# Two transforms moved inside the rounds of a spectral stage

## The chip, the cores and the metric

The kernel runs on one core of one Trainium2 chip. The metric is the device time in microseconds of one execution. Before the change three timed runs gave 10308.48, 10305.58 and 10307.53 us, a median of 10307.53.

## The reference, cut to what matters

The reference is a two-layer model on 4 images of 64 x 64 positions with 128 channels, in float32. Layer 0 is a selective scan in four directions and a mixture of experts; layer 1 is a mixing of sums and a spectral layer. Only the last one is touched:

```
def _stu_conv(phi, u, n):                        # n = 8192
    Vf = rfft(phi, n=n, axis=0)                  # 16 filters of 4096 taps
    Uf_p, Uf_m = rfft(u, n=n, axis=1), rfft(u * sgn3, n=n, axis=1)
    U_plus  = irfft(Vf[None, :, :, None] * Uf_p[:, :, None, :], n=n, axis=1)[:, :sl]
    ...
out = einsum('btkd,k,kde->bte', U_plus, s, Mpp) + einsum('btkd,k,kde->bte', U_minus, s, Mpm)
```

So a sequence of 4096 tokens is convolved with 16 filters, the results (once plain, once with alternating signs) go through one 128 x 128 matrix for each filter, and all are summed.

## The kernel before

The kernel turns the order round. For each frequency the 32 filter values and the 32 matrices are first combined into one 128 x 128 matrix, and the transformed tokens are multiplied by that. `spectrum()` does this for all frequencies, as the last stage but one. The stages before it (scans with pieces of other work dealt between them, the experts, the first part of the transform in `to_slots`) end at about 8736 us; `endings()` follows and does the last part of the inverse transform.

`spectrum()` is a loop of 32 rounds, `i = 0 ... 31`; each handles two slots (`FB = 2`) of 64 frequencies. A round issues these parts:

- `load(i + 2)` and `load_back(i - 1)`: loads, all from SyncE's queue (L1461, L1464, L1466, L1546, L1551).
- `taps_of(i)` makes the matrices, in 16 steps (`C // 8`). A step is eight matmuls with 32 rows (L1495) into a pair of PSUM buffers, and two copies of 128 x 1024 elements from these into `wt`, one with the elements woven (L1506), one plain (L1509).
- `forward(i + 1)`: the second part of the forward transform of the next round's tokens. For each slot there are four matmuls (L1474) and a copy into `ut` through the helper at L1456. Both slots share one PSUM buffer.
- `backward(i - 1)`: the first part of the inverse transform of the previous round's product. It is four matmuls of 512 columns (L1559) into one PSUM buffer, one copy into `zo`, and two stores to `zd` (L1564).
- `product(i)`: eight groups of 16 matmuls (L1524), tokens times matrices, each group followed by a copy into `zs`; every second copy is followed by four stores to `zf` (L1538).

`forward` and `backward` do not stand before or after `taps_of` but inside it. A dictionary `between` holds, for a step's number, a function that `taps_of` calls behind that step's copies (L1510).

Three things set the order and the waits around this.

First, buffers. All matmuls of the stage write to one pool of four PSUM buffers, `sp_ps` (L1436), each of two banks. `taps_of` takes two for a step, `forward` and `backward` one each, `product` one for each group. `wt` has one buffer (L1444): the first copies of a round wait until `product` of the round before has read it, and `product` reads all of it. `ut`, `vt`, `u1`, `fq`, `zq` and `gq` have two buffers, `zo` one and `zs` three.

Second, the copies. `copy()` (L1451) hands them out in turn to ScalarE and VectorE. A round has 32 + 2 + 1 + 8 = 43, an odd number; so in one round VectorE takes the first copy of each step and in the next ScalarE does. In what follows these are V rounds and S rounds.

Third, the framework orders each engine's instructions by a plan of its own, close to the program's order but not the same. VectorE and ScalarE work off their copies in that order, and SyncE its loads and stores.

Of the kernel before, what the change touches and what calls it, by code (L numbers as in the profile page):

```python
# [18 lines left out]
B, H, W, C = 4, 64, 64, 128  # L19
# [82 lines left out]
def kernel(  # L102
# [1330 lines left out]
    def spectrum():  # L1433

        with tc.tile_pool(name="sp", bufs=2) as sp, tc.tile_pool(
# [12 lines left out]
            def banks():  # L1448
                return sps.tile([P, 2, 512], F32, name="sp_ps", tag="ps")
# [5 lines left out]
            def out(dst, src):  # L1455
                copy()(dst, src)  # L1456

            def load(i):
                vt[i] = sp.tile([P, FB, 2 * BP], F32, name="vt")
                for g in range(4):  # L1460
                    nc.sync.dma_start(vt[i][g * KK : (g + 1) * KK], vd[:, FB * i : FB * (i + 1)])  # L1461
                for q in range(FB * i, FB * (i + 1)):
                    u1[q] = sp.tile([P, B, C], F32, name="u1")
                    nc.sync.dma_start(u1[q], ud[q])  # L1464
                    fq[q] = sp.tile([P, 2 * BP], F32, name="fq")
                    nc.sync.dma_start(fq[q], fq_d[q])  # L1466

            def forward(i):
                ps = banks()
                ut[i] = sp.tile([P, FB, BP, 2, B], F32, name="ut")  # L1470
                for s in range(FB):
                    q = FB * i + s
                    for b in range(B):
                        nc.tensor.matmul(  # L1474
                            ps[:, s, b * 2 * BP : (b + 1) * 2 * BP],
                            u1[q][:, b, :],
                            fq[q],
                            start=True,
                            stop=True,
                        )  # L1480
                    out(
                        ut[i][:, s].rearrange("d m u b -> d b (m u)"),
                        ps[:, s].rearrange("d (b n) -> d b n", b=B),
                    )

            def taps_of(i, between):
                for j in range(C // 8):
                    pair = [banks(), banks()]
                    for t in range(2):
                        for g in range(4):  # L1490
                            rows = slice(g * KK, (g + 1) * KK)
                            bank = pair[g // 2][:, g % 2]
                            woven = bank.rearrange("d (n t) -> d t n", t=2)[:, t]
                            plain = bank[:, t * 256 : (t + 1) * 256]
                            nc.tensor.matmul(  # L1495
                                woven if (g // 2 + j) % 2 else plain,
                                taps[rows, j, t, :],
                                vt[i][rows].rearrange("k s n -> k (s n)"),
                                start=True,
                                stop=True,  # L1500
                            )
                    for h in range(2):
                        dst = wt[:, 2 * j + h]
                        if (h + j) % 2:
                            src = pair[h].rearrange("d g (n t) -> d n g t", t=2)
                            copy()(dst.rearrange("d n (g t) -> d n g t", g=2), src)  # L1506
                        else:
                            src = pair[h].rearrange("d g (t n) -> d n (g t)", t=2)
                            copy()(dst, src)  # L1509
                    if j in between:  # L1510
                        between[j]()

            def product(i):
                for s in range(FB):
                    q = FB * i + s
                    for m in range(0, BP // 4, 4):
                        if m % 8 == 0:
                            zs = sp.tile([P, BP // 8, 2, C], F32, name="zs", bufs=3)
                        ps = banks()
                        for k in range(4):  # L1520
                            w0 = ut[i][:, s, 4 * (m + k) : 4 * (m + k) + 4]
                            for g in range(4):
                                n = 2 * (s * BP + 4 * (m + k) + g)
                                nc.tensor.matmul(  # L1524
                                    ps[32 * g : 32 * g + 32, k // 2, (k % 2) * 256 :][:, 0:256],
                                    w0.rearrange("d m u b -> d (m u b)"),
                                    wt[:, :, n : n + 2, :].rearrange("d a w e -> d w a e"),
                                    start=True,
                                    stop=True,
                                )  # L1530
                        out(
                            zs[:, m % 8 : m % 8 + 4].rearrange("z m w e -> z (m w e)"),
                            ps.rearrange("z k n -> z (k n)"),
                        )
                        if m % 8 == 0:
                            continue
                        for g in range(4):
                            nc.sync.dma_start(  # L1538
                                zf[q].rearrange("(m g) z n -> z g m n", g=4)[:, g, m - 4 : m + 4],
                                zs[40 * g : 40 * g + 8].rearrange("z m w e -> z m (w e)"),  # L1540
                            )

            def load_back(i):
                for q in range(FB * i, FB * (i + 1)):
                    zq[q] = sp.tile([P, B, 2, C], F32, name="zq")
                    nc.sync.dma_start(  # L1546
                        zq[q].rearrange("k b w e -> k (b w e)"),
                        zf[q].rearrange("m (u b) n -> (m u) (b n)", u=2),
                    )
                    gq[q] = sp.tile([P, 2, 2 * BP], F32, name="gq")  # L1550
                    nc.sync.dma_start(gq[q], gq_d[q])  # L1551

            def backward(i):
                ps = banks()
                zo = sp.tile([P, FB, B * C], F32, name="zo", bufs=1)
                for s in range(FB):
                    q = FB * i + s
                    for w in range(2):
                        nc.tensor.matmul(  # L1559
                            ps[:, s, :], gq[q][:, w, :], zq[q][:, :, w, :], start=(w == 0), stop=(w == 1)  # L1560
                        )
                out(zo, ps)
                for s in range(FB):
                    nc.sync.dma_start(  # L1564
                        zd[FB * i + s].rearrange("r p b e -> (r p) (b e)"), zo[:, s, :]
                    )
# [5 lines left out]
            for i in range(n):  # L1572
                between = {}
                if i + 2 < n:
                    load(i + 2)
                if i + 1 < n:
                    between[5] = lambda: forward(i + 1)
                if i >= 1:
                    load_back(i - 1)
                    between[10] = lambda: backward(i - 1)  # L1580
                taps_of(i, between)
                product(i)
            load_back(n - 1)
# [71 lines left out]
    with ExitStack() as c0:  # L1655
# [113 lines left out]
        for s in range(-5, total + 2):  # L1769
            i = max(s, 0) // N  # L1770
# [138 lines left out]
    side.pop("pool").close()  # L1909
    weights.close()  # L1910
    spectrum()
    endings()

# [73 lines left out]
```

## Time and profile before

| | us |
|---|---|
| median of three runs | 10307.53 |
| the profiled execution's own time | 10298.26 |
| its span in the trace | 10296.2 |
| up to 8736 (all before the spectral stage) | 8736.0, TensorE's granted clock 0.79 |
| 8736 to 10139 (the spectral stage) | 1403.0, clock 0.99; TensorE busy 1272.8, VectorE 816.5, ScalarE 694.4, GpSimd 0 |
| 10139 to the end (`endings`) | 157.2, clock 0.76, DMA engines busy 91% |
| one L1495 / L1524 / L1474 / L1559 matmul instruction in the trace | 0.374 / 0.379 / 0.275 / 0.592 |
| a `wt`, `zs` or `zo` copy on VectorE / on ScalarE | 1.22 / 1.01 |
| a `ut` copy on either | 1.06 |

The profile is one execution taken by the hardware profiler. Time in it is counted from the start of its span. A line of its views names the start, the length, the engine, the source line, the operation, what is written and read, how many instructions were merged, and, in brackets, how long the engine had been idle and what ended that. TensorE appears as PE, VectorE as DVE, ScalarE as ACT, GpSimd as POOL, SyncE's queue as SPq. Each float32 matmul shows as two records, so eight matmuls appear as x16. Matmuls overlap, so the time of a group is less than the sum of its records.

### The profile page before, as it was taken

The page shows a single profiled execution, that of the slowest core. Times are in us where ns is not written, and L with a number is a line of the kernel's source. Part 1 is how long each engine was busy: PE and PEld are TensorE (multiplying, and loading weights), DVE is VectorE, ACT ScalarE, POOL GpSimd, SP SyncE. Part 2 cuts the span into 40 slices and gives each one's busy share as a digit, 9 for nine tenths or more (in the row PEclk, how much of TensorE's full clock was granted, in tenths as well). Part 3 has the DMA queues.
Part 4 walks back from the last instruction along what each step waited for, and adds up shares of the span by engine and source line. Part 5 has one row for each costly group of instructions (what it writes and reads, how often), then busy time and mean ns, then how long its engine had stood idle before and what let it go on. Part 6 is the DMA issues. An engine that isn't in the chain of part 4 may idle for free. (4 is left out here: it accounts for less than half of the span.)

```text
span 10296.2 us, 137906 instructions
## 1 busy us (share of the span) xinstructions
PE 7631.4 (74%) x45570; PEld 4960.9 (48%) x45570; DVE 8537.4 (83%) x7103; ACT 6159.3 (60%) x11847; POOL 6493.4 (63%) x5948
## 2 busy tenths in 40 slices
PE   7676777667767767787767776767777767999996
PEld 3444444445543545444544554543555445666662
DVE  0899999989999999998999999999999951555553
ACT  4665766656755566675765666765576644554551
POOL 1677777878877778877877788877788741000000
PEclk9787787768777878788878887868877776999998
DMA  2556556657656645656756656756646663233336
GB/s 90 169 170 207 178 187 212 191 180 225 196 172 202 214 155 174 200 180 207 250 173 225 202 162 218 232 167 219 213 155 199 193 215 95 80 87 86 87 87 161
DMA packets 941918, 1806.03 MB, mean 175 GB/s; under 512 B 88184, under 2 KB 506648, under 8 KB 937624
## 3 DMA queue, kind: packets, MB, share of 16 engines
q1 hardware_dynamic: 941208, 1797.22, 54.7%
q8 instruction: 366, 6.00, 0.2%
q14 instruction: 344, 2.82, 0.1%
HBM read 1554.66 MB, written 242.22 MB: 175 GB/s over the span
## 5 line engine op out<-in xcount | busy, mean ns | idle before, releaser
L1846 POOL TENSOR_TENSOR hh<-hh,bc 128x1024 f32<-128x1024 f32 x2048 | 4886.8, 2386 | 384.9 <-DVE hh L1836 151.0
L1836 DVE TENSOR_TENSOR_SCAN hh<-da,hst,db 128x512 f32<-128x512 f32 x3584 | 4393.1, 1267 | 281.5 <-PE y L1872 30.1
L1872 PE MATMUL y<-ident,hh 128*128 128x128 f32 x16384 | 2723.2, 321 | 1524.8 <-POOL hh L1846 1429.0
L1786 ACT ACTIVATE da<-dl,aneg 128x512 f32<-128x512 f32 x4096 | 2781.8, 717 | 1543.7 <-DVE hh L1836 1531.2
L1872 PEld LDWEIGHTS y<-ident,hh 128*128 128x128 f32 x16384 | 2259.0, 166 | 2486.4 <-POOL hh L1846 1868.7
L1830 DVE TENSOR_TENSOR db<-du,bc 128x1024 f32<-128x1024 f32 x1920 | 2365.2, 1232 | 97.7 <-ACT du L1767 19.2
L1845 POOL COPY hst<-hh 128x2 f32<-128x2 f32 x1792 | 365.9, 204 | 1037.9 <-DVE hh L1836 937.0
L1495 PE MATMUL sp_ps<-vt,taps 32*128 32x256 f32 x8192 | 638.1, 405 | 52.3 <-DVE wt L1509 19.7
L1836 DVE TENSOR_TENSOR_SCAN hh<-da,db 128x512 f32<-128x512 f32 x512 | 597.0, 1208 | 38.4 <-PE y L1872 5.8
L1495 PEld LDWEIGHTS sp_ps<-vt,taps 32*128 32x128 f32 x8192 | 438.1, 185 | 245.6 <-DVE wt L1506 63.0
L440 PE MATMUL cv_ps<-xh,diag 128*128 128x512 f32 x1152 | 525.8, 599 | 1.8 <-ACT sg_v L382 0.9
L1524 PE MATMUL sp_ps<-wt,ut 128*32 128x256 f32 x8192 | 448.7, 379 | 45.2 <-DVE wt L1509 22.7
L1830 DVE TENSOR_TENSOR db<-dx,bc 128x1024 f32<-128x1024 f32 x128 | 179.3, 1401 | 297.9 <-POOL dx L1714 285.8
L1686 PE MATMUL dt_ps<-dts,dtw 8*128 8x512 f32 x512 | 378.9, 844 | 52.8 <-ACT sg_v L382 35.5
L1506 DVE COPY wt<-sp_ps 128x1024 f32<-128x1024 f32 x257 | 314.4, 1223 | 123.6 <-PE sp_ps L1495 112.2
L1509 DVE COPY wt<-sp_ps 128x1024 f32<-128x1024 f32 x255 | 311.3, 1221 | 121.9 <-PE sp_ps L1495 115.4
L1711 PE MATMUL dl_ps<-ex,ident 128*128 128x512 f32 x512 | 315.3, 704 | 121.9 <-POOL ex L1705 121.8
L1524 PEld LDWEIGHTS sp_ps<-wt,ut 128*32 128x32 f32 x8192 | 318.7, 110 | 172.6 <-ACT wt L1506 28.7
L1705 POOL TENSOR_TENSOR ex<-ex,dx 128x1024 f32<-128x1024 f32 x128 | 302.0, 2360 | 107.6 <-DMA bc<-bc_d 72.5
L1509 ACT COPY wt<-sp_ps 128x1024 f32<-128x1024 f32 x257 | 260.2, 1012 | 178.4 <-PE sp_ps L1495 169.4
L1456 DVE COPY zs<-sp_ps 128x1024 f32<-128x1024 f32 x128 | 156.5, 1222 | 241.8 <-PE sp_ps L1524 235.6
L1714 POOL TENSOR_TENSOR dx<-dl,xc 128x1024 f32<-128x1024 f32 x128 | 302.5, 2363 | 69.3 <-ACT dl L1712 62.8
(289 smaller groups left out, 9915.6 us busy)
## 6 DMA issues: line engine op xcount, KB each, us to landing
bc<-bc_d SPq DMA_DIRECT2D x2048, 512.0 KB
xc<-xc_d SPq DMA_DIRECT2D x128, 512.0 KB
y_d<-ys SPq DMA_DIRECT2D x128, 512.0 KB
w1t<-in_w_dram SPq DMA_DIRECT2D x96, 512.0 KB
w2t<-in_w_dram SPq DMA_DIRECT2D x192, 256.0 KB
xc_x<-xc_d SPq DMA_DIRECT2D x64, 512.0 KB
yk<-y_d SPq DMA_DIRECT2D x128, 256.0 KB
yk<-y_d SPq DMA_DIRECT2D x256, 128.0 KB
```

The lines of the kernel that those rows point to most:

```text
L440: nc.tensor.matmul(ps, diag[:, h, t, :], xh[:, 8 * g + dy : 8 * g + dy + 8, dx : dx + W], start=(t == 0), stop=(t == 8),)
L1495: nc.tensor.matmul(woven if (g // 2 + j) % 2 else plain, taps[rows, j, t, :], vt[i][rows].rearrange("k s n -> k (s n)"), start=True, stop= ...
L1509: copy()(dst, src)
L1524: nc.tensor.matmul(ps[32 * g : 32 * g + 32, k // 2, (k % 2) * 256 :][:, 0:256], w0.rearrange("d m u b -> d (m u b)"), wt[:, :, n : n + 2, ...
L1686: nc.tensor.matmul(ps, dtw[:, k, h * P : (h + 1) * P], dts, start=True, stop=True)
L1711: nc.tensor.matmul(ps, ident, t[:, h], start=t is dl, stop=t is w)
L1786: i_act = nc.scalar.activation(das[t][:, h, :], sizes[t // N][0][:, h, :], AF.Exp, scale=aneg[:, tk, h, t % N : t % N + 1],)
L1830: nc.vector.tensor_mul(db, src, bcs[s][:, 0:1, :].to_broadcast([P, 2, SC]))
L1836: i_dve = nc.vector.tensor_tensor_scan(o, d0, d1, init, ALU.mult, ALU.add)
L1845: nc.gpsimd.tensor_copy(hsts[t // N][:, :, t % N], hhs[t][:, :, last])
L1846: i_pool = nc.gpsimd.tensor_mul(hhs[t], hhs[t], bcs.pop(t)[:, 1:2, :].to_broadcast([P, 2, SC]))
L1872: i_pe = nc.tensor.matmul(ys[c][:, q, h, :], hhs[t][:, h, q * P : (q + 1) * P], ident, is_transpose=True, start=(n == 0 and k > 0 and q % ...
```

## The change

In the loop of `spectrum()` two keys of `between` change. `forward(i + 1)` is called behind step 0 of `taps_of(i)` in place of step 5, and `backward(i - 1)` behind step 15, the last, in place of step 10. What the two functions do is as it was.

```diff
@@ -1574,10 +1574,10 @@
                 if i + 2 < n:
                     load(i + 2)
                 if i + 1 < n:
-                    between[5] = lambda: forward(i + 1)
+                    between[0] = lambda: forward(i + 1)
                 if i >= 1:
                     load_back(i - 1)
-                    between[10] = lambda: backward(i - 1)
+                    between[C // 8 - 1] = lambda: backward(i - 1)
                 taps_of(i, between)
                 product(i)
             load_back(n - 1)
```

In the order in which the changed program issues TensorE's instructions, the second half of the forward stands among the matmuls of step 1. On SyncE's queue the `vt` loads now stand ahead of the `gq` loads and the `zd` stores; before, they stood behind them.

## The prediction

> **What bounds the kernel now.** I read the whole page first, then busy time by stretch, then three views of one pair of rounds: TensorE in order of time, the chain that ended last, VectorE in order of time. The change sits in the spectral stage, which is 32 rounds. Cutting at the starts of `product` gives the stage its clock and load:
>
> ```profile
> 8767.36:9071.22 303.86, 277.14 (x3753) 188.66 (x3753) 177.96 (x150) 152.31 (x151) 0.00 (x0) 1.00 0.31 86
> 9374.05:9677.80 303.75, 278.10 (x3753) 189.81 (x3754) 178.06 (x150) 152.42 (x151) 0.00 (x0) 0.99 0.32 86
> ```
>
> Columns: the stretch, its length, then busy time of TensorE matmuls, weight loads, VectorE, ScalarE, GpSimd, then granted clock, DMA share, GB/s. In seven rounds (303.86 us) TensorE is busy 277.14 us; about 9% of the stage is TensorE waiting, and that is all that reordering can win. Clock and DMA leave room.
>
> TensorE in order of time, one round (start, duration, line, tiles, count, idle before it):
>
> ```profile
> 9027.65 14.02 PE L1524 MATMUL sp_ps<-wt,ut 128*32 128x256 f32 x256 [1.42 <-DVE wt L1509]
> 9041.60 1.15 PE L1495 MATMUL sp_ps<-vt,taps 32*128 32x256 f32 x16
> 9043.85 6.97 PE L1495 MATMUL sp_ps<-vt,taps 32*128 32x256 f32 x80 [1.10 <-ACT wt L1509]
> 9050.75 1.16 PE L1474 MATMUL sp_ps<-fq,u 128*128 128x128 f32 x8
> 9051.83 0.70 PE L1495 MATMUL sp_ps<-vt,taps 32*128 32x256 f32 x4
> 9053.05 1.16 PE L1474 MATMUL sp_ps<-fq,u 128*128 128x128 f32 x8 [0.51 <-ACT ut L1456]
> ...
> 9060.12 3.70 PE L1559 MATMUL sp_ps<-zq,gq 128*128 128x512 f32 x8
> ...
> 9071.22 1.07 PE L1524 MATMUL sp_ps<-wt,ut 128*32 128x256 f32 x16 [1.41 <-DVE wt L1506]
> ```
>
> Each step of `taps_of` is one 1.15 us group. Every `product` starts after a wait of 1.41 us: its matmuls read all of `wt`, so they need the last step's copies. The chain shows the same at the other kind of round:
>
> ```profile
> 9025.15 1.23 DVE wt L1506
> 9026.38 1.14 DVE wt L1509
> 9027.52 0.14 issue
> 9027.65 14.02 PE sp_ps L1524 x256
> ```
>
> Within the steps VectorE sets the pace. Its copies in the last round:
>
> ```profile
> 10084.68 1.23 DVE L1509 COPY wt<-sp_ps 128x1024 f32<-128x1024 f32 x1 [0.67 <-PE sp_ps L1495]
> 10085.82 1.22 DVE L1506 COPY wt<-sp_ps 128x1024 f32<-128x1024 f32 x1
> ...
> 10095.66 1.22 DVE L1506 COPY wt<-sp_ps 128x1024 f32<-128x1024 f32 x1
> ```
>
> Ten steps, nine distances, 10.98 us: 1.22 us a step, where TensorE needs 1.15. With four PSUM buffers TensorE is at most two steps ahead, so it is held to that pace (waits of 0.16 to 0.18 us in the trace).
>
> I follow a round by the start of VectorE's copy of each step. V rounds (VectorE copies the first half of a step) and S rounds (ScalarE does) alternate. From the end of `product` to the next start, with the starts that VectorE's timeline gives:
>
> V, 8998.70 to 9027.65, copies of steps 1, 5, 6, 10, 11, 15 at 9002.27, 9007.19, 9011.32, 9016.24, 9021.37, 9026.29: first even-paced copy (step 1) at 3.57; steps 1-5 4.92; across the forward 4.13; 6-10 4.92; across the backward 5.13; 11-15 4.92; then 1.36 to `product`. Sum 28.95.
>
> S, 9041.67 to 9071.22, the same at 9045.94, 9050.86, 9055.32, 9060.23, 9064.93, 9069.85: 4.27 + 4.92 + 4.46 + 4.91 + 4.70 + 4.92 + 1.37 = 29.55.
>
> Against 1.23 for an ordinary step, the forward costs 2.90 (V) and 3.23 (S), the backward 3.90 and 3.47, the end 1.36.
>
> **What the Trainium skill says.** "Perfetto Trace Analysis", section Optimization Strategy: the same gap repeating on the engine that should be saturated can mean too few buffers. This trace agrees: the gap of 1.41 us recurs, behind a one-buffer `wt`. "TensorE: Matmul & The Clock Gate", section Architectural detail: ScalarE and VectorE are strictly first in, first out; only weight loads may be pulled ahead on TensorE. The trace agrees: a `zs` copy whose matmuls ended at about 8996.95 (seventh of `product`'s eight groups, 1.75 us each from 8984.68) ran at 9000.95, behind a `wt` copy. So the built order decides. Same page, section What's actually happening: idleness lowers the clock, activity restores it. The stage already has 0.99 to 1.00; no spell worth mentioning is there to win.
>
> **The change, part by part.** No instruction is added or removed: 8 forward matmuls and 2 copies, 4 backward matmuls, 1 copy and their loads and stores move. The built program confirms the move: after step 0's eight matmuls comes the first half of the forward, then a few matmuls of step 1, the second half, and steps 1 to 15 unbroken; then the backward, then `product`. The copies still alternate; V and S rounds remain.
>
> *Forward, from step 5 to step 0.* Its first half takes the PSUM buffer of step 0's first copy, so it inherits the 1.10 to 1.31 us wait that step 1 had. V: step 0's matmuls end at 1.09, copy from 1.11 for 1.24, TensorE at 2.39. Half to half is 2.30 (9050.75 to 9053.05; the second waits for the first's `ut` copy): 4.69. To VectorE's next step copy was 1.87 (9009.45 to 9011.32); one matmul more is already done, 0.14: step 1's copy at 6.42 instead of 3.57. That is 2.85, for the 2.90 saved. S: ScalarE's copy ends at 2.13, TensorE 2.17, second half 4.47, plus 2.27 (9053.05 to 9055.32, VectorE's `ut` copy in between) gives 6.74, so 2.47 for 3.23.
>
> *Steps 1 to 15 unbroken.* 14 distances of 1.23 are 17.22. The backward in the middle gave VectorE a rest of 2.8 us before `zo` or 3.5 us; it is not needed, since the pace is the copy's own.
>
> *Backward, from step 10 to the end.* TensorE reached it 0.03 (V) or 0.11 (S) before VectorE's copy of step 10 began, and passed on after 3.60 to 3.63. So V: 6.42 + 17.22 - 0.03 + 3.60 = 27.21, S: 6.74 + 17.22 - 0.11 + 3.63 = 27.48. VectorE's last `wt` copy ends at 24.87 or 25.19, over 2.2 us before `product`: the 1.36 us is hidden behind the backward. Without that cover it comes back in full. `zo`'s copy (1.01 or 1.23) moves into `product`'s start, where neither copy engine has work for 1.7 us; its buffer is wanted by `product`'s fourth group, 3 x 1.75 = 5.3 us in. What is late next is VectorE's pace, 1.23 against 1.15, and the forward's wait for its own copy.
>
> *Loads and stores on SyncE's queue.* Loads of `u1` and `fq` for the next forward issue once this one has read its buffers, now right behind the `zf` stores (SyncE's timeline: issued until 9004.42, +5.7), a round early as before. `zq` stands behind them: issued at 9011.48, +12.8, it moves to about +8 and is wanted at +23.6. The page "DMA: Bandwidth & Descriptors", section Latency and other measured facts, puts a DMA's fixed cost at about 2 us; here `zd` landed 2.35 us after its issue. So the waits of 4.3 us in all for `zq` end. The `vt` loads now pass ahead of `gq` and `zd`; `gq` waits for the backward to free its buffers and is wanted a round later. `zd` issues about 1.3 us into `product`, the first `zf` store about 4.5 us in: no clash. GpSimd has no work here.
>
> **Sum.** The 30 rounds between `product`'s starts at 8767.36 and 10066.39 took 1299.03. After: mean of 27.21 and 27.48, plus 14.02, is 41.37, times 30 is 1241.1: 57.9 saved. The last round has no forward: 40.24 becomes 4.27 + 17.22 - 0.11 + 3.63 + 14.02 = 39.03, 1.2 saved. Round 0 has no backward and keeps its last wait; its moved forward meets loads issued at 8742.4, so I count 0, from -1 to +1. In all 59.1. Profiled execution: 10298.26 - 59.1 = 10239. The median of the runs is 9.27 above that execution: 10307.53 - 59.1 = **10248**.
>
> Unknown: the start of the even pace, +-0.35 a round (a matmul group's handover, seen only at other places), +-11 us; the pace over 15 steps, seen over ten, +-0.02 a step, +-9 us.
>
> **Rivals.** *The pace slips (10287).* If TensorE fed every copy late, at 1.32 (the longer distance between copies, 10085.82 to 10087.14) in place of 1.23, a round gives back 1.26, 39 us. Against: the last round's 1.22. Chance 0.06.
>
> *The wait only changes place (10307).* If the copies rather than TensorE set the round, the backward's 3.6 us would just be paid elsewhere. It needs the last copy to end more than 3.6 us behind TensorE; it ended 1.4 behind. That the change has no effect at all is excluded by the built order. Chance 0.04.
>
> *Slower: the clock (10500).* Fewer gaps mean a denser TensorE, 91% to about 96% busy (277 of 304 - 14), and full 128x128 backward next to `product`. The page shows tenths of 7 and 8 in earlier slices. TensorE alone sets `product`, backward and forward, 19.7 us a round; at clock c that grows by 31 x 19.7 x (1/c - 1), and below 0.93 the steps grow too. At 0.92 the gain is used up; at 0.8 it costs 153 + 103 us, net 197 slower. Against: 0.99 to 1.00 over the stage at 91% busy, with matmuls that use a quarter of the array. Chance 0.04.
>
> **Numbers.** Forecast 0.86, the rivals 0.06, 0.04, 0.04. Its own bounds, 11 + 9 + 1 each way, give 10228 to 10269; the rivals outside are 0.14, so I keep 10228 to 10270. A measurement of this kernel tells 0.2%, 20.6 us, from no change. Faster: 0.92; same: 0.04; slower: 0.04.
>
> **What would show it.** After: starts of `product` 41.2 to 41.5 us apart; no wait on a `wt` copy before it; the forward's first half waiting for step 0's copy; VectorE's copies 1.23 apart over 15 steps; no wait for `zq`; clock 0.99 or more. Wrong if the copies run at 1.3, if `product` waits for `zo` or `zf`, or if the clock falls below 0.95.

## The result, and the profile after

The changed kernel takes 10262.27 us (median of 6 runs, 10256.13 to 10272.76), the kernel before 10308.01 us (median of 6, 10305.58 to 10320.57). The ratio is 0.9955, with a 95% interval of 0.9943 to 0.9967: 45.7 us faster, where the prediction said 59.1. The profiled execution of the changed kernel took 10262.52 us, with a span of 10260.5 us.

A measure without the scatter of the rest of the program is the time between the start of `product` 0 and the start of `product` 31, read in each trace. Before it was 1339.28 us, after it is 1294.52 us: 44.76 us saved in the 31 rounds between. (Between the two profiled executions only 35.7 us are saved: in the profile of the changed kernel, `product` 0 starts 8.83 us later, 8776.19 in place of 8767.36, most of it in stages whose code is the same.)

TensorE in order of time, one pair of rounds (start, duration, line, tiles, count, idle before it and what ended it):

```profile
8986.61 14.02 PE L1524 MATMUL sp_ps<-wt,ut 128*32 128x256 f32 x256
9000.56 1.15 PE L1495 MATMUL sp_ps<-vt,taps 32*128 32x256 f32 x16
9003.02 1.16 PE L1474 MATMUL sp_ps<-fq,u 128*128 128x128 f32 x8 [1.31 <-DVE wt L1509]
...
9005.33 1.16 PE L1474 MATMUL sp_ps<-fq,u 128*128 128x128 f32 x8 [0.48 <-DVE ut L1456]
9006.41 17.94 PE L1495 MATMUL sp_ps<-vt,taps 32*128 32x256 f32 x234
9024.47 3.70 PE L1559 MATMUL sp_ps<-zq,gq 128*128 128x512 f32 x8
9028.10 14.02 PE L1524 MATMUL sp_ps<-wt,ut 128*32 128x256 f32 x256
...
9044.29 1.16 PE L1474 MATMUL sp_ps<-fq,u 128*128 128x128 f32 x8 [1.10 <-ACT wt L1509]
```

The forward (L1474) now stands right behind step 0 and has taken over the wait for step 0's copy, 1.31 or 1.10 us. Steps 1 to 15 run through in this round, then the backward (L1559), and `product` (L1524) starts behind it without any wait. The chain of what ended last says the same of the end of a round: VectorE's copy of step 14, the backward, `product`.

```profile
9023.19 1.24 DVE wt L1509
...
9024.47 3.70 PE sp_ps L1559 x8
9028.17 13.95 PE sp_ps L1524 x256
```

VectorE's copies of steps 1 and 15 in the first of the two rounds:

```profile
9007.18 1.23 DVE L1506 COPY wt<-sp_ps 128x1024 f32<-128x1024 f32 x1 [1.91 <-PE sp_ps L1495]
...
9024.39 1.22 DVE L1506 COPY wt<-sp_ps 128x1024 f32<-128x1024 f32 x1
```

Fourteen distances in 17.21 us are 1.23 a step, as forecast (17.22). TensorE's waits over the stage, from 8776 to 10060 us (wait and what it was for: us in total, times, longest):

```profile
PE sp_ps L1474 <- DVE wt L1509: 19.7, 15, 1.3
PE sp_ps L1474 <- ACT wt L1509: 16.5, 15, 1.2
PE sp_ps L1524 <- DVE wt L1509: 1.4, 1, 1.4
```

Before, in the same stretch, `product` waited 41.0 us for `wt` in 29 rounds; one such wait is left, in round 0, which has no backward.

The stage by stretch, cut at the starts of `product` (length, then busy time of TensorE matmuls, weight loads, VectorE, ScalarE, GpSimd, then granted clock, DMA share, GB/s):

```profile
8776.19:9069.65 293.46, 277.98 (x3756) 178.17 (x3760) 178.69 (x150) 151.51 (x150) 0.00 (x0) 0.99 0.32 88
```

TensorE's work in seven rounds is what it was, 278 us, in 293.46 us in place of 303.86.

So far the round is what was predicted. The periods from `product` to `product` are not all alike, though: 41.49 us three times, then 42.80, again and again. A round of 42.80, TensorE in order of time behind step 0:

```profile
8918.73 1.16 PE L1474 MATMUL sp_ps<-fq,u 128*128 128x128 f32 x8 [1.31 <-DVE wt L1509]
8919.82 0.73 PE L1495 MATMUL sp_ps<-vt,taps 32*128 32x256 f32 x6
8921.03 2.08 PE L1474 MATMUL sp_ps<-fq,u 128*128 128x128 f32 x8 [0.48 <-DVE ut L1456]
```

The second half of the forward takes 2.08 us where it takes 1.16 in the other rounds. Cut at the place where this begins, the busy times by stretch (columns as above) show why:

```profile
8917.66:8921.07 3.41, 1.86 (x15) 1.34 (x15) 3.20 (x3) 0.86 (x1) 0.00 (x0) 1.00 0.08 12
8921.07:8924.48 3.41, 3.41 (x21) 3.03 (x24) 0.15 (x1) 1.07 (x1) 0.00 (x0) 0.50 0.62 140
```

For 3.41 us TensorE had half its clock. The trace has eight such windows between `product` 0 and `product` 31, in rounds 1, 4, 8, 12, 16, 20, 24 and 28, each 18.6 to 18.8 us behind the start of the `product` before it, that is, at the forward's second half. I call such a window at half clock a spell. In the same stage of the kernel before there was one. A spell made its round 1.31 us longer (the first, 1.6).

**What is to be explained** is thus 14.7 us: 59.1 forecast, 44.4 found (44.76, less 0.39 that round 0 took longer). Two theories of the spells went into the experiments.

- *Idle window.* The forward behind step 0 puts two of TensorE's waits, 1.31 us for step 0's copy and 0.48 for the forward's own, into one stretch of 3.4 us with only 1.86 us of work. Where that lines up with the window over which the clock's gate, the part that halves the clock, counts TensorE's activity, the next window has half the clock.
- *Density (the rival, as in the prediction).* TensorE has fewer gaps over the whole stage than before, and the throttle answers that.

The Trainium skill, "TensorE: Matmul & The Clock Gate", section What's actually happening, says that the gate watches a window of 3413 ns that runs freely and that the clock is either half or whole. This trace agrees: every spell is 3.41 us at 0.50, and from the spell of round 4 to that of round 28 are 1003.52 us, 294 times 3.4133.

### The profile page after: what moved, and what is told of

It reads as the page before. It is cut to its first block, busy times and chain, and to the rows that moved or that the text cites. A ratio compares the mean times of both kernels' runs of the same rounds, so it can differ in the third digit from the quotient of the medians.

```text
span 10260.5 us, 137964 instructions
## 1 busy us (share of the span) xinstructions
PE 7621.4 (74%) x45570; PEld 4890.3 (48%) x45570; DVE 8536.1 (83%) x7103; ACT 6160.7 (60%) x11847; POOL 6493.8 (63%) x5948
## 5 line engine op out<-in xcount | busy, mean ns | idle before, releaser
L1524 PE MATMUL sp_ps<-wt,ut 128*32 128x256 f32 x8192 | 448.7, 379 | 1.4 <-DVE wt L1509 1.4
L1524 PEld LDWEIGHTS sp_ps<-wt,ut 128*32 128x32 f32 x8192 | 264.7, 110 | 193.9 <-issue 23.5
```

The source lines that it names most:

```text
L1524: nc.tensor.matmul(ps[32 * g : 32 * g + 32, k // 2, (k % 2) * 256 :][:, 0:256], w0.rearrange("d m u b -> d (m u b)"), wt[:, :, n : n + 2, ...
```

## The experiments

Each is the changed kernel with the edit that is shown, which is cut to its main lines ("..." marks a gap); where a heading or a row says "the same" or names two things, the edits are put together. "31 rounds" is the time from `product` 0 to `product` 31 in the profile. The kernel before was timed again beside each group of runs (medians 10310.38, 10305.64 and 10309.78 us), and the ratios are to those.

| kernel | 31 rounds, us | half-clock spells in them | mean round (first 30), us | median, us | ratio to before, 95% interval |
|---|---|---|---|---|---|
| before | 1339.28 | 1 | 43.30 | 10308.01 | |
| the changed kernel | 1294.52 | 8 | 41.85 | 10262.27 | 0.9955 (0.9943 to 0.9967) |
| forward alone moved | 1360.78 | 24 | 44.02 | 10330.54 | 1.0020 (1.0012 to 1.0028) |
| backward alone moved | 1294.57 | 0 | 41.85 | 10264.40 | 0.9956 (0.9944 to 0.9969) |
| four matmuls into the wait | 1283.72 | 0 | 41.49 | 10253.41 | 0.9951 (0.9938 to 0.9963) |
| halves of the forward together | 1273.07 | 0 | 41.13 | 10240.13 | 0.9934 (0.9921 to 0.9946) |
| the same, ahead of step 0 | 1284.65 | 9 | 41.52 | 10254.99 | 0.9948 (0.9934 to 0.9963) |
| together, one copy | 1262.00 | 0 | 40.77 | 10234.05 | 0.9929 (0.9914 to 0.9944) |
| ahead of step 0, one copy | 1270.30 | 2 | 41.04 | 10240.56 | 0.9934 (0.9917 to 0.9950) |
| the same, copies shared 5 to 4 | 1266.98 | 0 | 40.95 | 10233.34 | 0.9928 (0.9913 to 0.9943) |
| changed kernel, four `zs` | 1252.26 | 0 | 40.47 | 10211.59 | 0.9904 (0.9889 to 0.9919) |
| together, one copy, four `zs` | 1226.32 | 0 | 39.62 | 10190.78 | 0.9883 (0.9869 to 0.9898) |
| ahead, one copy, four `zs` | 1227.99 | 0 | 39.67 | 10194.66 | 0.9887 (0.9871 to 0.9904) |
| the same, shared 5 to 4 | 1241.66 | 1 | 40.15 | 10209.07 | 0.9900 (0.9885 to 0.9914) |

The spells are counted in one execution of each kernel. The median of the runs less the 31 rounds lies between 8959 and 8972 us in all fourteen kernels, so the one profile speaks for the runs to about 10 us.

### One half of the change at a time

```diff
-                    between[C // 8 - 1] = lambda: backward(i - 1)
+                    between[10] = lambda: backward(i - 1)
```

> Only the forward is moved (behind step 0); the backward stays behind step 10. From the rows of before and after: V rounds 6.55 + 11.07 (9 x 1.23) + 5.13 + 4.92 + 1.36 = 29.03 us from the end of a product to the next start, S rounds 6.74 + 11.07 + 4.70 + 4.92 + 1.37 = 28.80; mean period 42.93 against 43.30 before, so some 10 to 11 us saved over the stage if the clock stays whole. Theory (the forward behind step 0 puts two waits of TensorE into one stretch of about 3.4 us, and the clock halves in the next stretch whenever its window lines up with that): 4 to 8 half-clock spells of 3.41 us again, each right behind step 0 of a round, each costing 1.3 us, so that 0 to 6 us are saved. Rival (the spells come because TensorE is denser): TensorE is hardly denser here than before, so at most one spell in the stage, as before, and the whole 10 us saved.

```diff
-                    between[0] = lambda: forward(i + 1)
+                    between[5] = lambda: forward(i + 1)
```

> Only the backward is moved (behind step 15); the forward stays behind step 5. V rounds 3.57 + 4.92 + 4.13 + 11.07 (9 x 1.23) - 0.03 + 3.60 = 27.26 us, S rounds 4.27 + 4.92 + 4.46 + 11.07 - 0.11 + 3.63 = 28.24; mean 27.75, with the product 41.77 a round; against 43.30 before 1.53 x 30 = 46 us saved, plus 1.2 in the last round. Theory (spells come from the forward behind step 0): no or one half-clock spell in the stage, all of the 47 us saved, about 10261. Rival (spells come from a denser TensorE): as dense as after, so some eight spells, about 11 us less saved, about 10272.

The forward alone made the kernel slower: 31 rounds take 21.50 us more than before, and the run is 0.2% longer, with the interval wholly above 1. There are 24 spells. The clock by stretch (columns as above) over the 31 rounds:

```profile
8778.38:10139.15 1360.77, 1247.11 (x16600) 861.00 (x16601) 786.33 (x665) 671.18 (x666) 0.00 (x0) 0.97 0.31 84
```

The rival's one spell is refuted: here TensorE is busy 1247 of 1361 us, 92%, hardly denser than before (1223.74 of 1339.28, 91%), with three times as many spells as after. The theory had the place of the spells right, but their number, 4 to 8, far too low, and so its 0 to 6 us saved are wrong too. The reason is in the periods: 44.24 to 44.36 us six times, then 42.9 twice, and again. With its spell of 1.4 us a round comes out just short of 13 windows of 3.413, 44.37 us; so the next round meets the window in nearly the same place, and the spells follow each other until the drift (18.5 us behind `product`'s start in the first of six, 18.8 in the last) carries the round out of step. In the changed kernel four rounds with one spell are 167.26 us, 49 windows. Without spells the forward alone would be worth what was expected: the undisturbed rounds are 42.9, against 43.30.

The backward alone has no spell, and its 31 rounds, 1294.57 us, are those of the whole change. Its S rounds are 42.32 and its V rounds 41.38 (expected, with 14.02 added: 42.26 and 41.28). TensorE is busy 1225.14 us of them, 95%, the share of the changed kernel (1224.80 of 1294.52), and still there is no spell: this is the plainest evidence against density. TensorE at the end of one round:

```profile
9013.13 3.70 PE L1559 MATMUL sp_ps<-zq,gq 128*128 128x512 f32 x8
9016.76 14.02 PE L1524 MATMUL sp_ps<-wt,ut 128*32 128x256 f32 x256
```

So all of the gain that was measured is the backward's. The forward's move is worth 0.36 us in an undisturbed round (41.85 - 41.49), 10.8 us in thirty, and the spells took 10.8 us back.

### Work in the wait

If a lack of work brings the spells, more work must end them. The four matmuls of step 0 that fill its second PSUM buffer are issued once more, behind the step:

```diff
+                    if j == 0 and 0 in between:
+                        for t in range(2):
+                            for g in (2, 3):
...
+                                nc.tensor.matmul(
+                                    woven,
+                                    taps[rows, j, t, :],
+                                    vt[i][rows].rearrange("k s n -> k (s n)"),
...
```

> The changed kernel, and behind step 0 its last four matmuls once more (same operands, same result), so that TensorE works 0.57 us of the wait for step 0's first copy, which lasts 1.1 to 1.3 us. The work that sets the round is untouched, TensorE only gets denser. Theory (too little work of TensorE in one window in front of the forward's second half halves the clock): the half-clock spells go, 8 down to at most 2, and the stage is 8 to 11 us shorter than that of the changed kernel, in spite of added work. Rival (denser TensorE brings the spells): as many spells or more, the stage as long as the changed kernel's or longer. Should the added four matmuls delay the second copy of step 0 by 0.57 us, up to 0.6 x 30 = 17 us are lost in either theory, seen as a later copy of step 1.

```profile
9000.52 1.03 PE L1508 MATMUL sp_ps<-vt,taps 32*128 32x256 f32 x8
9002.00 1.16 PE L1474 MATMUL sp_ps<-fq,u 128*128 128x128 f32 x8 [0.45 <-DVE wt L1522]
```

L1508 is the added work; the forward's wait is down from 1.31 to 0.45 us, and its start, 2.39 us behind the end of `product`, is where it was. No spell is left. The 30 rounds are 41.48 to 41.54 us, and the 31 rounds 10.80 us shorter than those of the changed kernel, though TensorE has more to do. The emptiest stretch of 3.41 us in a round now has TensorE busy for 71%, against 53% in the changed kernel. This is the cleanest of the runs: more work in that stretch, with the same pace around it, ends the spells, and 10.8 us is what they cost. (The run's median is 8.9 us lower; in this profile round 0, at the start of the stage, took 3.6 us more than in that of the changed kernel.)

### Halves together, and where the forward stands

```diff
                             stop=True,
                         )
+                for s in range(FB):
                     out(
```

> The changed kernel with the forward's eight matmul pairs of both halves issued together, and then its two copies: the second half no longer waits for the first half's copy (half to half 2.30 us before and after, now about 1.15). Theory: the start of the even pace comes up to 1.15 us earlier in every round with a forward, 30 x 1.15 = 34 us, if VectorE's pace does not take it up; and with one of the two waits gone from the stretch in front, the half-clock spells go too, another 10 us: 10217 to 10228. Rival (density): spells stay, 10228 or more. If the copies of the forward (two, on two engines, now back to back) hold up step 1's copies instead, less than half of the 34 us comes.

The spells went, and the round fell to 41.13 us, 0.36 below the undisturbed 41.49, where 1.15 was hoped for. TensorE and ScalarE in order of time, one round:

```profile
9002.94 2.05 PE L1474 MATMUL sp_ps<-fq,u 128*128 128x128 f32 x16 [1.31 <-DVE wt L1510]
...
9007.27 4.34 PE L1496 MATMUL sp_ps<-vt,taps 32*128 32x256 f32 x60 [0.78 <-ACT ut L1456]
```

```profile
9006.15 1.07 ACT L1456 COPY ut<-sp_ps 128x512 f32<-128x512 f32 x1 [3.41 <-DVE ut L1456]
```

The wait between the halves has moved behind step 1: ScalarE's copy of the second half starts only when VectorE's of the first has ended, and step 2 needs the buffer. As expected for that case, less than half came.

With one copy for both halves, still behind step 0 (the edit is to the run before):

```diff
-                for s in range(FB):
-                    out(
-                        ut[i][:, s].rearrange("d m u b -> d b (m u)"),
-                        ps[:, s].rearrange("d (b n) -> d b n", b=B),
-                    )
+                out(
+                    ut[i].rearrange("d s m u b -> d s b (m u)"),
+                    ps.rearrange("d s (b n) -> d s b n", b=B),
+                )
```

> As the run with both halves of the forward issued together, but one copy moves both halves (128x1024, 1.22 us by the rows of that size) in place of two of 1.07 that ran one behind the other. Theory: the second copy, which waited 1.07 for the first, held up TensorE by 0.78 us behind step 1 and ScalarE's copy of step 1, and so took back most of what issuing the halves together gave. Without it the even pace starts about 0.45 us earlier: 40.7 us a round against 41.13, 13 us less, about 10227, and no wait of TensorE for a forward copy over 0.2 us. Rival (VectorE has one longer copy in a row and sets the pace anyway): the round stays at 41.1. With an even number of copies in a round, V and S rounds no longer alternate.

40.77 us a round is the time expected, but for another reason than expected in part: the copy takes 1.96 to 1.99 us, not 1.22, and TensorE still waits 0.57 us for it behind step 1. What else became shorter is the wait in front of the forward, 1.10 in every round, since with an even number of copies ScalarE has step 0's first copy each time.

The forward ahead of step 0, with two copies and with one, and then with five of nine copies on ScalarE:

```diff
             def taps_of(i, between):
+                if -1 in between:
+                    between[-1]()
                 for j in range(C // 8):
...
-                    between[0] = lambda: forward(i + 1)
+                    between[-1] = lambda: forward(i + 1)
```

> As the run with both halves of the forward issued together, and the forward is put ahead of step 0 instead of behind it, right after product. Theory: the forward's wait of 1.1 to 1.3 us was for step 0's copy and has nothing to wait for here; its eight matmul pairs take 2.05 us, its two copies run one behind the other to about 4.2 us, VectorE's copy of step 1 starts at about 4.8 instead of 6.3: 4.8 + 17.22 + 3.63 + 14.02 = 39.7 us a round against 41.13, some 40 us less in all, about 10197; no half-clock spell. Rival: the wait only changes place, step 0 now waits 1.1 to 1.3 us for what product's last copies and the forward's copies hold, and the round stays within 0.3 us of 41.1.

> The forward ahead of step 0, its halves together, one copy for both. Theory: forward to 2.05 us, step 0 to 3.2, copies of step 1 from about 4.4: 4.4 + 17.22 + 3.63 + 14.02 = 39.3 us a round, so 55 us less than with the halves together behind step 0: about 10185. No half-clock spell, and no wait of TensorE over 0.3 us other than VectorE's pace. Rival: as with the forward ahead and two copies, a wait in front of step 0 instead, 40 us or more a round.

```diff
-                return nc.scalar.copy if side["e"] % 2 else nc.vector.tensor_copy
+                return nc.vector.tensor_copy if side["e"] % 9 % 2 else nc.scalar.copy
```

> The same, and of nine copies ScalarE takes five and VectorE four, in place of turns. Theory (VectorE's 1.23 a step sets the steps, TensorE alone would need 1.15): the steps run at TensorE's own 1.15 to 1.17, 15 x 0.06 to 0.08 = 0.9 to 1.2 us a round: 38.2 to 38.5 us a round, about 10155. Rival: the pairs of copies that ScalarE now does one behind the other make TensorE wait for a PSUM buffer as often as VectorE's pace did, and the round stays at that of the run before.

In the first two the rival was right, the wait only changed place: undisturbed rounds of 41.08 to 41.30 and of 40.94 us. The first has nine spells where none was expected. The wait now stands in the middle of step 0. TensorE and ScalarE with one copy:

```profile
9001.81 1.12 PE L1497 MATMUL sp_ps<-vt,taps 32*128 32x256 f32 x6
9003.93 19.21 PE L1497 MATMUL sp_ps<-vt,taps 32*128 32x256 f32 x250 [1.00 <-ACT ut L1456]
```

```profile
9001.92 1.96 ACT L1456 COPY ut<-sp_ps 128x1024 f32<-128x1024 f32 x1 [6.08 <-PE sp_ps L1474]
9003.68 1.05 ACT L1456 COPY zs<-sp_ps 128x1024 f32<-128x1024 f32 x1
```

A `zs` copy of the `product` that ended at 8999.83 runs at 9003.68, behind the forward's copy, on an engine that had been idle for 6.08 us. So its PSUM buffer is not free when step 0 needs a second one, and step 0 goes on at 9003.93, when the forward's copy ends (9003.88) and its buffer comes free. The changed kernel has the same late copy. Its VectorE:

```profile
9001.74 1.23 DVE L1509 COPY wt<-sp_ps 128x1024 f32<-128x1024 f32 x1 [5.00 <-PE sp_ps L1495]
9002.88 1.21 DVE L1456 COPY zs<-sp_ps 128x1024 f32<-128x1024 f32 x1
```

It is idle for 5.00 us, copies step 0, and only then the seventh group of a `product` whose seventh group was done at about 8998.9. This copy writes the fourth `zs` tile of the `product`, and with three buffers that needs the one whose stores come first. ScalarE's copy of the eighth group, into the same tile, ran at 9000.74, so the buffer was free by then; what holds the seventh is its place behind step 0's copy, which is fixed in the built order. Sharing the copies five to four brought 40.60, 40.84 and 41.39 us in turn, no better as a mean (40.95) than 40.94: ScalarE then has pairs of copies one behind the other, and its rival was right. In the last run below, sharing even costs 0.48 us a round (40.15 against 39.67), where the rival had allowed 0.2.

### Four zs buffers

```diff
-                            zs = sp.tile([P, BP // 8, 2, C], F32, name="zs", bufs=3)
+                            zs = sp.tile([P, BP // 8, 2, C], F32, name="zs", bufs=4)
```

> The changed kernel with four zs buffers in place of three, nothing else. With three, the seventh group of a product must wait for the stores of the first, so its copy is built behind step 0's copy on its engine, and its PSUM buffer comes free only then; the forward's first half takes another buffer and waits for it 1.10 to 1.31 us. Theory (that late copy is what the forward's first wait comes from, and the wait is what the half-clock spells come from): the copy runs right at the end of the product, the forward's first half starts at once behind step 0, the copy of step 1 starts some 1.2 us earlier, so 30 x 1.2 = 36 us, and the spells go, 10.8 us more: the stage about 47 us shorter than the changed kernel's 1325.6, about 10215 for the run. Rival (the wait is for ScalarE's and VectorE's work as such): the wait stays over 0.8 us in front of the forward or behind it, and less than 15 us come.

> The run with one copy for the forward behind step 0, with four zs buffers. Theory: no wait in front of the forward, TensorE is through it at 3.2 us from the product's end; the even pace starts about 1.2 us earlier: 39.4 to 39.7 us a round against 40.77, 33 to 41 us less than with three: about 10197. Rival: the copy of both halves, 1.96 us on either engine, holds step 2 by as much, and the round stays over 40.3.

> The run with the forward ahead of step 0 and one copy, with four zs buffers. Theory: the wait of 1.00 us in the middle of step 0 was for the seventh group's buffer, whose copy stood behind the forward's; it goes, VectorE's copy of step 1 starts at about 4.5 us: 4.5 + 17.22 + 3.7 + 14.02 = 39.4 us a round against 40.94, 46 us less: about 10195. Rival: the wait moves to step 1, for the forward's own buffer, and the round stays over 40.3.

> The same, with five of nine copies on ScalarE. Theory: with the steps at TensorE's own 1.15 to 1.18 in place of 1.23, 38.4 to 38.8 us a round, 18 to 30 us below the run before: about 10170. Rival: ScalarE's pairs of copies cost as much as VectorE's pace, and it stays within 0.2 us a round of the run before.

In the changed kernel with four buffers, TensorE and ScalarE:

```profile
9023.61 1.15 PE L1495 MATMUL sp_ps<-vt,taps 32*128 32x256 f32 x16
9024.69 1.16 PE L1474 MATMUL sp_ps<-fq,u 128*128 128x128 f32 x8
9026.99 1.16 PE L1474 MATMUL sp_ps<-fq,u 128*128 128x128 f32 x8 [0.52 <-ACT ut L1456]
```

```profile
9022.06 1.01 ACT L1456 COPY zs<-sp_ps 128x1024 f32<-128x1024 f32 x1 [2.44 <-DMA zf<-zs]
9024.79 1.01 ACT L1509 COPY wt<-sp_ps 128x1024 f32<-128x1024 f32 x1 [1.71 <-PE sp_ps L1495]
```

The seventh group's copy runs at 9022.06, ahead of step 0's, the forward follows step 0 without a wait, and there is no spell. The 31 rounds are 42.3 us shorter than with three buffers: 10.8 for the spells, 30 x (41.49 - 40.47) = 30.6 for the wait, and 0.85 in the last round. So the wait that the forward "inherits" is not the price of step 0's copy as such; it comes from a store buffer that was one too few, by way of the late copy. The expectation, 47 us and 10215, was near: 10211.59.

The next two show what is left: 39.62 us a round with the forward whole behind step 0, 39.67 with it ahead, so that with the wait gone the place no longer matters. Both are within 0.3 us of what was expected. The fastest, 10190.78 us, is 1.2% below before, more than twice the gain of the change. TensorE is busy 1173.56 of its 1226.32 us, 96%, and in the run with work in the wait 1239.12 of 1283.72, 97%, against 95% in the changed kernel; neither has a spell, so the density theory fails once more.

**What stays open** is what exactly the gate counts. In the changed kernel and with the forward alone, every window ahead of a spell has TensorE busy for 52 to 61%; but the kernel before has windows of 1.81 us busy in 3.40 (53%), made up of steps and `product` alone, with no spell behind them, and the kernel with the forward ahead of step 0 has nine spells behind windows of 65%, where other windows of 65% have none. With the halves of the forward together the emptiest windows are busy for 61%, and none brings a spell. So the busy time of a window does not decide alone; whether the kind of work matters beside it is not shown, since no run here separates the two. The single spells elsewhere are not explained: the kernel before has one in round 17, behind a window busy for 68%, the forward ahead with one copy has two (at the start of `product` 0 and in round 1), and the last row has one at the start of `product` 0.

## Why the prediction was right, and where it was not

**The end of the round: right.** "the 1.36 us is hidden behind the backward" held: `product` waits for `wt` in round 0 alone. The backward starts 0.08 us behind the copy of step 15 (V; -0.03 forecast) and passes on after 3.63. Done alone, this part saved 44.7 us of the some 47 it was given.

**Steps 1 to 15 at VectorE's pace: right.** 17.21 us for 17.22. The rival in which TensorE feeds the copies late is out, and so is the one in which the wait only changes place, for the backward. For the forward it came true in a milder form.

**The forward behind step 0: right in the undisturbed round, to 0.1 us.** Its first half starts 2.39 us behind the end of `product` (2.39 forecast), the second 2.31 later (2.30). VectorE's copy of step 1 starts at 6.55 in V rounds, not 6.42: the matmul that was "already done, 0.14" gave nothing. With the backward's start, 0.11 later than forecast, this makes V rounds 27.47 from the end of `product` to the next start, for 27.21; S rounds have 6.74 as forecast, and 27.46 for 27.48. Periods of 41.49 in place of 41.37 on average are 3.6 us in thirty rounds.

**The last round: right**, 39.01 for 39.03. **The queues: right**; TensorE's waits in the stage no longer have a row for `zq`.

**The step that failed** is the sentence on the clock, "The stage already has 0.99 to 1.00; no spell worth mentioning is there to win". It asked only whether the change could win clock, and the rival on the clock asked only whether a denser TensorE could lose it. Neither looked at the single window of 3.4 us. The forward's first half was costed as a wait of 1.31 us inherited from step 1, "2.85, for the 2.90 saved", and at once followed by its own half-to-half wait; that the two now fall into one window was in the numbers and not seen. The term is the forward's: 12 us forecast (30 x (41.77 - 41.37)), 10.8 in undisturbed rounds, nothing after eight spells of 1.31 to 1.6 us, 10.8 us together. With 3.6 for the start of the even pace and of the backward and 0.4 for round 0 that is the whole of the 14.7 us missing. The mechanism of the change was right, and its size was off by this. The sign that was named, "clock 0.99 or more", held (0.99) and did not show the loss.

**That 10262.27 lies inside 10228 to 10270 owes something to luck.** The bounds had no term for the clock. The 10.8 us fit in, with less than 8 us to spare, because the rest of the sum came out within 4 us of the forecast, where 11, 9 and 1 us had been allowed.

**What was in sight and not followed.** The prediction took the repeating gap of 1.41 us in front of `product` for a sign of too few buffers, those of `wt`. It did not ask the same of the other repeating gap, the 1.10 to 1.31 us behind step 0, though it saw a `zs` copy run at 9000.95, some 4 us behind its matmuls. There `zs` was the buffer that was short: a fourth one took 42.3 us off the 31 rounds of the changed kernel.

The section of the Trainium skill that the prediction had quoted for "idleness lowers the clock" was the right one, and not applied. The page's section HAM oscillation speaks of gaps over about 3.4 us; here no single gap in the window ahead of any of the eight spells was over 1.31 us, and the measurement decides. Its next section, A second HAM failure mode, has short idle times between groups of matmuls, as buffers in PSUM go round, bringing the clock down again and again; that is what these traces show, with 24 spells at worst.

## What to carry to other kernels

Before moving a short piece of TensorE work next to a wait, add up TensorE's idle time within one clock window (3.4 us here), not only its waits one by one; a stage with a mean clock of 0.99 can lose a fifth of a gain to it (10.8 of 55.6 us here), and a repeating loop can lock on to the window. Where an inserted piece inherits a wait, follow the buffer it waits for to the copy that frees it and ask why that copy is late: here one more store buffer was worth nearly as much as the change itself. Measure each half of a change alone; this one's forward half, by itself, made the kernel slower.

## What the runs showed that was not expected

- Loops lock on to the clock window: with the forward alone, the spells of six rounds in eight are 44.37 us apart, 13 windows; in the changed kernel four rounds with one spell are 167.26 us, 49 windows.
- Added work made the kernel faster: four matmuls more in each of 31 rounds, 10.8 us less.
- The copy of both forward halves, 128x1024, writes every fourth element of `ut` and took 1.96 us on ScalarE and 1.97 on VectorE, where the copies of the same size into `wt` and `zs` take 1.01 and 1.22. Each of the two copies of 128x512 took 1.06 to 1.08.
